# Inner seven-product forms for three aggregation products, and attention's side work in two blocks a unit

## The chip, the cores and the metric

The kernel runs on one core of a Trainium2 chip, in one launch. The metric is device time in microseconds. The kernel before takes 3564.32 us (median of three runs, 3564.18 to 3565.26). Engines are named as in the profile: PE is TensorE's matmuls, PEld its weight loads, DVE is VectorE, ACT ScalarE, POOL GpSimd, and SP the engine that issues most DMAs.

## The reference

```python
# x: (8, 2048, 256), adj: (2048, 2048), all float32
A_norm = A + eye(n)
deg = sum(A_norm, 0) + sum(A_norm, 1) - diagonal(A_norm)
A_hat = A_norm * rsqrt(deg)[:, None] * rsqrt(deg)[None, :]
agg = einsum('nm,bmd->bnd', A_hat, features)
h = relu(batchnorm(agg @ W1.T + b1, g1, be1))        # 512 columns
out = batchnorm(h @ W2.T + b2, g2, be2)              # 256 columns
x = layernorm(x + out)
qkv = x @ W                                          # 4 heads of 64
scores = einsum('bhid,bhjd->bhij', q, k) / sqrt(64) + mask   # -inf where adj == 0
x = layernorm(x + einsum('bhij,bhjd->bhid', softmax(scores), v))
```

## The kernel before

Everything is float32; one matmul is two records in the profile. There are three stages on TensorE: the aggregation with the first linear map (59 to about 1000 us), the second linear map (to about 1222 us), and attention (to the end).

**Aggregation.** The transposed adjacency is kept in SBUF in quarters `T[k, (i, j)]` of 128 x 8 x 512: i and j name halves of the 2048 nodes (contraction and output), and k counts the two 512-column slices of each half (`HT` is 8, `NK` 2, `CH` 512). A unit is (k, a pair of batches b and b + 1, d): d is the half of x's 256 columns. There are 16 units, d innermost; the two units of one (k, b) are called a pair here. In a unit the two batches and the two contraction halves make a 2 x 2 block product, done with seven products instead of eight: `product` (L360 ff.) runs 8 matmuls of 128 x 512 into one PSUM tile of the pool `psa` (four buffers). The stationary sides are the loaded x tiles `S[v, i, j]`, scaled on POOL by `scale` (L333), and their sums `S[v, 1]` to `S[v, 4]` (`s1` to `s4`, L346 to L358, on POOL). The moving sides are the quarters and their sums `T[k, 2]` to `T[k, 4]` (`t2` to `t4`, L371 to L379, on DVE, once for each k). ACT copies the first product out of PSUM, DVE adds the others, POOL multiplies the results by a row of 1/sqrt(deg) (`dbc`). x tiles and sums lie in places `x0` to `x8` (`Form`), given out in the order in which they came free.

After the d = 1 unit, `linear` (L404 ff.) does the first linear map for the two batches, again with seven products: for batch b + 1 at once, for batch b after the next unit's first product (`later`). Its forms (`linear_form`, L402) are made on POOL. The results lie in two tiles h0 and h1 and go to DRAM as `h_d`.

At the change of k (`turn`) the other four quarters are fetched from DRAM, the mask of one quarter and the sums t1 to t4 are made on DVE. `mask_of` writes the 0/1 mask of a quarter to DRAM three more times for each k.

**Attention.** 64 units (batch, pair of heads, 512 query rows) of 16 steps. In each step TensorE does the scores of three steps ahead (L933, four 64x64 matmuls) and the weighting of the values of this step (L963, four more); DVE adds the mask (L945), ACT takes the exponential (L951), and POOL adds the exponentials up (L973 as DMA, L975, L984, L986). Between these, side work is put in at steps given by hand, `at_step(unit, step, function)`: the sums of the unit before (`finish_sums`, L1004), their transposition (L1018), the turning of the output (`finish_turn`, L1031), q, k and v projections (L867, L881) of coming units, and for the next batch the transposition of y and x (`norm` L801, `turn` L830). A task with a whole-number step comes before the mask and the exponential of its step, one with a fraction after them.

**Order.** On all five engines (four in attention) instructions stay in the order in which the program writes them. An instruction that waits holds up all that stand behind it on its engine, on SP's queue of DMAs too.

Of the kernel before, what the change touches and what calls it, by code (L numbers as in the profile page):

```python
# [26 lines left out]
def tile_gcn_then_masked_attention(  # L27
# [15 lines left out]
    nc = tc.nc  # L43
# [88 lines left out]

    HT = NT // 2
# [23 lines left out]
    free = [f"x{i}" for i in range(9)]  # L157
# [24 lines left out]
    def mask_of(k, ij):  # L182

        i, j = ij
        m8 = bp.tile([P, HT, CH], U8, name="m8")
        nc.vector.tensor_scalar(m8, T[k, ij], 0.0, None, op0=ALU.is_equal)
        if i == j:
            for q in range(TPC):
                m = k * TPC + q
                nc.vector.tensor_copy(  # L190
                    m8[:, m, q * P : (q + 1) * P], mdiag[:, i * HT + m, :]
                )
        mask_out(k, ij, m8)
# [4 lines left out]
    with tc.tile_pool(name="bt7", bufs=1, side="right") as bp7, tc.tile_pool(  # L198
# [7 lines left out]
        m8 = bp.tile([P, HT, CH], U8, name="m8")  # L206
# [92 lines left out]
        mask_out(0, (0, 1), m8)  # L299

# [3 lines left out]
    with tc.tile_pool(  # L304
        name="psa", bufs=4, space=PSUM
    ) as psa, tc.tile_pool(name="psh", bufs=4, space=PSUM) as psh, tc.manual_schedule(engines=ALL4):
        for j in range(2):
            lp.tile([P, NH, CH], F32, name=f"h{j}")
# [95 lines left out]
        def linear(k, b, ag, i):  # L404

            cs = [(b + i) * NCH + j * NK + k for j in range(2)]
            lo, hi = (lp.tile([P, NH, CH], F32, name=f"h{j}") for j in range(2))
# [7 lines left out]
            def plus(h, f, p, u):  # L415
                nc.vector.scalar_tensor_tensor(
                    h[:, f, :], p, b1s[:, f : f + 1], u, op0=ALU.add, op1=ALU.add
                )

            for s, p in products((0, 0), ag[i, 0][:, 0, :]):  # L420
                nc.scalar.copy(lo[:, 2 + s, :], p)  # L421
            linear_form(ag, i, 3)
            for s, p in products((0, 1), ag[i, 0][:, 1, :]):
                plus(lo, s, p, lo[:, 2 + s, :])
            linear_form(ag, i, 4)
            for s, p in products(2, G[i, 2]):
                nc.vector.tensor_add(hi[:, s, :], p, lo[:, 2 + s, :])
            for s, p in products(3, G[i, 3]):
                nc.vector.tensor_add(hi[:, 2 + s, :], p, hi[:, s, :])
            for s, p in products((1, 1), G[i, 4]):  # L430
                plus(lo, 2 + s, p, hi[:, 2 + s, :])
            nc.sync.dma_start(h_d[cs[0]], lo)
            for s, p in products(1, G[i, 1]):
                plus(hi, 2 + s, p, hi[:, 2 + s, :])
                nc.vector.tensor_add(hi[:, s, :], p, hi[:, s, :])
            for s, p in products(4, ag[i, 1][:, 1, :]):
                plus(hi, s, p, hi[:, s, :])
            nc.sync.dma_start(h_d[cs[1]], hi)
            for c, h in zip(cs, (lo, hi)):
                for f in range(NH):  # L440
                    nc.vector.bn_stats(st1[:, f, c, :], h[:, f, :])
# [9 lines left out]
        nc.gpsimd.tensor_sub(W1[4], W1[0, 1], W1[2])  # L451
        ag = None
        for v, (k, b, d) in enumerate(units):
# [9 lines left out]

            def do_p6():
                p6 = product(S[v, 2], T[k, 2])
                nc.vector.tensor_add(u2, p6, u1)

# [5 lines left out]
            if not last:  # L473
                nb, nd = units[w][1:]
                S[w, 0, 0] = load_form(nb, 0, nd)
                S[w, 1, 0] = load_form(nb + 1, 0, nd)
                S[w, 1, 1] = load_form(nb + 1, 1, nd)
# [10 lines left out]
            if turn:  # L488
                fetch(k + 1, (0, 1), 4)
# [3 lines left out]
            if first:  # L493
                p3 = product(S[v, 4], T[k, (1, 1)])
                do_p6()
            if not last:
                S[w, 0, 1] = load_form(nb, 1, nd)
                for ij in ((0, 0), (1, 0), (1, 1)):
                    scale(w, *ij)
            if turn:  # L500
                fetch(k + 1, (1, 1), 2)
            if d and not last:
                for i in range(2):
                    linear_form(ag, i, 1)
            p7 = product(S[v, 3], T[k, 3])
            nc.vector.tensor_add(u3, p7, u2)
            if turn:
                mask_of(k + 1, (0, 1))
                t1 = T[k + 1, (0, 1)]
                nc.vector.tensor_sub(t1, t1, T[k + 1, (0, 0)])  # L510
            if not (last or turn):
                s1(w)
                s2(w)
                s3(w)
            p4 = product(S[v, 1, 1], T[k, 4])
            nc.vector.tensor_add(c21, p4, u3)
            nc.gpsimd.tensor_mul(c21, c21, dbc[0][:, 0, :])
            if turn:
                fetch(k + 1, (1, 0), 6)
                t2(k + 1, 5)  # L520
            if not last:
                scale(w, 0, 1)
                if not turn:
                    s4(w)
            p5 = product(S[v, 1], T[k, (0, 1)])
            nc.vector.tensor_add(c22, p5, u3)
            nc.vector.tensor_add(u2, p5, u2)
            nc.gpsimd.tensor_mul(c22, c22, dbc[0][:, 1, :])
            if d and not last:
                linear_form(ag, 1, 2)  # L530
            if turn:
                t3(k + 1, 1)
            if not first:
                p3 = product(S[v, 4], T[k, (1, 1)])
            nc.vector.tensor_add(c12, p3, u2)
            nc.gpsimd.tensor_mul(c12, c12, dbc[0][:, 1, :])

            n = v % (len(units) // NK)
            if n in (2, 4, 6):
                mask_of(k, ((0, 0), (1, 0), (1, 1))[n // 2 - 1])  # L540
            if last:
                break
            if d:
                linear(k, b, ag, 1)
                linear_form(ag, 0, 2)
                if turn:
                    t4(k + 1, 3)
                    s1(w)
                    s2(w)
                later = [lambda k=k, b=b, ag=ag: linear(k, b, ag, 0)]  # L550
                if turn:
                    later += [lambda w=w: s3(w), lambda w=w: s4(w)]
# [18 lines left out]
        for name, size in (  # L571
            ("h1", [P, NH, CH]), ("dbc", [P, 2, CH]), ("w1f", [P, 4, H // 2])
        ):
            t = lp.tile(size, F32, name=name).rearrange("p a b -> p (a b)")
            for i in range(size[1] * size[2] * 2 // N):
                tx = t[:, i * N // 2 : (i + 1) * N // 2].rearrange("p (t d) -> p t d", d=D)
                nc.sync.dma_start(
                    tx, x[0, len(x0) * CH : (len(x0) + 1) * CH].rearrange("(t p) d -> p t d", p=P)
                )
                x0.append(tx)  # L580
        wt = lp.tile([P, NH, CH], F32, name=f"h0")
        w2s = wt[:, :2, :].rearrange("p a b -> p (a b)").rearrange("p (f o) -> p f o", f=NH)
        w2f = wt[:, 2:, :].rearrange("p a b -> p (a b)").rearrange(
            "p (n f o) -> p n f o", n=4, f=2
        )
        nc.sync.dma_start(w2s, w2t.rearrange("(c p) f -> p c f", p=P))
# [3 lines left out]
        def w_half(i, j):  # L590
            return w2s[:, 2 * j : 2 * j + 2, i * P : (i + 1) * P]

        W = {ij: w_half(*ij) for ij in HALVES}
        W[1], W[2], W[3], W[4] = (w2f[:, n] for n in range(4))
# [172 lines left out]
    class Layer1Input:  # L767
# [27 lines left out]

        def turn_y(self, b, c, half, pm):
# [41 lines left out]
        def emit_stats(self, b, c, half):  # L838
# [14 lines left out]
        def project(self, b, hp, c, which, k_on_act=False):  # L853
# [10 lines left out]
            pm = self.psum.tile([P, CH], F32, name="pm")  # L864
# [34 lines left out]
    def attention():  # L899


        with tc.tile_pool(
# [178 lines left out]

            per_b = HP * NCH
            for u in range(NU):
                b, hp, c = units[u]
                at_step(u + 1, 6, finish_sums, u)
                at_step(u + 1, 10, finish_turn_sums, u)
                at_step(u + 1, 10.2, finish_turn, u)
                at_step(u + 1, 10.3, finish, u, 0)
                at_step(u + 1, 11.1, finish, u, 1)
                if u == NU - 2:  # L1090
                    for half in range(2):
                        at_step(u + 1, 11.3 + half, inp.emit_stats, b, c, half)
                        at_step(u + 1, 14 + half, inp.emit, b, c, half)
                    at_step(u + 1, 12.5, inp.root, b, c)
                elif u == NU - 1:
                    for half in range(2):
                        at_step(u + 1, 10.4 + half, inp.emit_stats, b, c, half)
# [4 lines left out]
                    at_step(u + 1, 10.45, count_bad)  # L1102
                elif hp == HP - 1:
                    for half in range(2):
                        at_step(u + 1, 12.5 + 1.5 * half, inp.emit_stats, b, c, half)
# [5 lines left out]
            PROJECT = (0.2, 6.1, 10.1)  # L1111

            def project_at(u, b, hp, c):
                for w in range(3):
                    at_step(u, PROJECT[w], inp.project, b, hp, c, w)

            for b in range(B):
                u0 = b * per_b
                if b:
                    project_at(u0, b, 0, NCH - 1)  # L1120
                for c in range(NCH):
                    project_at(u0 + 1 + c, b, 1, c)
# [7 lines left out]
                    at_step(u, 6.2, inp.norm, b + 1, c, 0)  # L1130
                    at_step(u + 1, 0.1, inp.norm, b + 1, c, 1)
                    at_step(u + 1, 3, inp.root, b + 1, c)
                    for half in range(2):
                        at_step(u + 1, 7 + half, inp.apply, b + 1, c, half)
                        at_step(u + 1, 13 + 0.2 * half, inp.turn, b + 1, c, half)
# [13 lines left out]
            for c in (2, 3):  # L1149
                at_step(c - 1, 3.1, inp.project, 0, 0, c, 0)  # L1150
# [76 lines left out]
    def attention_with_maxima():  # L1227

        with tc.tile_pool(name="full", bufs=2) as ap_, tc.tile_pool(
# [9 lines left out]
            for b in range(B):  # L1239
# [55 lines left out]
                for c in range(NCH):  # L1295
                    for half in range(2):
                        inp.emit_stats(b, c, half)
# [53 lines left out]
```

## Time and profile before

| what | us |
|---|---|
| median of three runs | 3564.32 |
| profiled execution: device time | 3566.12 |
| profiled execution: span | 3564.3 |
| L363 aggregation products, PE busy | 774.8 |
| L412 first linear map, PE busy, its three largest groups | 76.8, 76.7, 26.3 |
| L933 scores / L963 values, PE busy | 1062.9 / 1074.2 |
| L867 and L881 projections, PE busy | 250.8 and 125.1 |
| 59 to 995 us: POOL busy / DVE busy | 434 / 338 |
| 1247 to 3552 us: POOL busy / DVE busy | 1698 / 1576 |

A group's line reads: line, engine, operation, output <- inputs, shapes, count | busy us, mean ns of one | idle before it and who ended that. A timeline line reads: start, duration (both us), engine, line, operation, count. Rows of PE in the timeline overlap a little, since matmuls are pipelined; the distance of two starts is what a group takes.

### The profile page before, as it was taken

What the parts mean: (1) busy time and instruction counts of PE and PEld (TensorE: products, weight loads), DVE (VectorE), ACT (ScalarE), POOL (GpSimd) and SP (SyncE); (2) the same over time, 40 slices, a digit from 0 to 9 for tenths busy, and PEclk for the clock granted to TensorE, in tenths of its full rate; (3) what the DMA queues carried; (4) which work ended last, traced back from release to release, by engine and by line L of the source; (5) the groups of instructions that cost most, each with busy time, mean ns of one, the idle gap of its engine ahead of it and who ended that gap; (6) DMA issues with size and microseconds to landing.
All of it is one profiled execution on the core that took longest, in us unless ns stands there. A gap on an engine that the chain in (4) does not pass through costs nothing. (4 is left out here: it accounts for less than half of the span.)

```text
span 3564.3 us, 55375 instructions
## 1 busy us (share of the span) xinstructions
PE 3527.1 (99%) x22483; PEld 1461.0 (41%) x22483; DVE 2113.4 (59%) x3128; ACT 1575.4 (44%) x1952; POOL 2330.5 (65%) x1588
## 2 busy tenths in 40 slices
PE   8999999999999999999999999999999999999998
PEld 5444444444444433433343433343443334343332
DVE  6224343442346656766766776676676676677666
ACT  5000000000045455665665565565566566566555
POOL 4544364435357656777777787777677777777777
PEclk9999999999999999999999999999999999999999
DMA  9122342231256445666575566566656556555655
GB/s 342 54 77 76 95 153 78 71 95 39 84 217 249 156 84 109 128 126 123 110 149 117 115 129 134 113 133 129 118 124 136 114 117 145 115 117 115 122 107 121
DMA packets 197577, 440.16 MB, mean 123 GB/s; under 512 B 14128, under 2 KB 121152, under 8 KB 186944
## 3 DMA queue, kind: packets, MB, share of 16 engines
q0 software_dynamic: 64656, 239.37, 35.3%
q1 hardware_dynamic: 132048, 196.11, 16.2%
q8 instruction: 178, 2.92, 0.3%
q10 hardware_dynamic: 608, 1.06, 0.1%
q14 instruction: 87, 0.71, 0.1%
HBM read 126.62 MB, written 75.51 MB: 57 GB/s over the span
## 5 line engine op out<-in xcount | busy, mean ns | idle before, releaser
L945 DVE SCALAR_TENSOR_TENSOR prob<-mask,st 128x1024 f32<-128x1024 uint8 x1024 | 1239.0, 1215 | 434.6 <-PE st L933 358.6
L951 ACT ACTIVATE prob<-prob 128x1024 f32<-128x1024 f32 x1024 | 1081.2, 1056 | 913.4 <-DVE prob L945 836.6
L963 PE MATMUL out_ps<-prob,v 64*64 64x512 f32 x8192 | 1074.2, 595 | 3.6 <-DVE ot L991 2.6
L933 PE MATMUL st<-qt,kt 64*64 64x512 f32 x8192 | 1062.9, 589 | 0.1
L986 POOL TENSOR_TENSOR acc<-acc,prob 128x1024 f32<-128x1024 f32 x317 | 825.6, 2604 | 5.5 <-DMA prob<-prob 0.6
L363 PE MATMUL pa<-t,x 128*128 128x512 f32 x1792 | 774.8, 594 | 2.8 <-ACT t L239 2.8
L973 POOL DMA_DIRECT2D prob<-prob x447 | 403.6, 928 | 565.4 <-PE out_ps L963 453.4
L933 PEld LDWEIGHTS st<-qt,kt 64*64 64x64 f32 x8192 | 312.5, 133 | 566.7 <-issue 527.0
L363 PEld LDWEIGHTS pa<-t,x 128*128 128x128 f32 x1792 | 341.4, 191 | 432.9 <-issue 428.7
L963 PEld LDWEIGHTS out_ps<-prob,v 64*64 64x64 f32 x8192 | 290.8, 133 | 542.4 <-issue 470.5
L975 POOL TENSOR_TENSOR acc<-acc,prob 128x1024 f32<-128x1024 f32 x126 | 298.1, 2366 | 7.5
L867 PE MATMUL pm<-x1t,wq 128*128 128x512 f32 x512 | 250.8, 613 | 0.7 <-ACT x1t L836 0.7
L492 POOL TENSOR_TENSOR ag<-ag,dbc 128x512 f32<-128x512 f32 x16 | 20.2, 1264 | 314.7 <-DVE ag L491 287.2
L472 ACT COPY ag<-pa 128x512 f32<-128x512 f32 x16 | 9.4, 588 | 450.0 <-PE pa L363 434.0
L421 ACT COPY h<-ph 128x512 f32<-128x512 f32 x28 | 16.4, 585 | 416.7 <-PE ph L412 416.7
L984 POOL TENSOR_TENSOR acc<-prob 128x1024 f32<-128x1024 f32 x64 | 170.7, 2667 | 3.0 <-DMA prob<-prob 3.0
L762 ACT ACTIVATE x<-x,ln_nm,ln_rs 128x256 f32<-128x256 f32 x256 | 137.6, 586 | 7.5 <-POOL ln_nm L758 7.5
L1039 DVE SCALAR_TENSOR_TENSOR x<-pm,ri,x 128x64 f32<-128x64 f32 x512 | 109.6, 277 | 43.6 <-PE pm L1031 43.6
L867 PEld LDWEIGHTS pm<-x1t,wq 128*128 128x128 f32 x512 | 86.9, 189 | 118.2 <-issue 111.6
L881 PE MATMUL pm<-wq,x1t 128*128 128x128 f32 x1024 | 125.1, 275 | 0.0
L881 PEld LDWEIGHTS pm<-wq,x1t 128*128 128x128 f32 x1024 | 119.4, 192 | 2.5 <-ACT x1t L836 1.7
L991 DVE TENSOR_TENSOR ot<-out_ps,ot 128x512 f32<-128x512 f32 x64 | 44.3, 692 | 123.9 <-ACT ot L990 123.9
(158 smaller groups left out, 2863.5 us busy)
## 6 DMA issues: line engine op xcount, KB each, us to landing
prob<-prob POOLq DMA_DIRECT2D x447, 512.0 KB, 4.9
x<-in_x_dram SPq DMA_DIRECT2D x92, 512.0 KB, 6.5
h_d<-h SPq DMA_DIRECT2D x28, 1024.0 KB, 4.3
t<-h_d SPq DMA_DIRECT2D x28, 1024.0 KB, 8.2
a<-in_adj_dram SPq DMA_DIRECT2D x16, 1024.0 KB, 5.4
y_d<-ag SPq DMA_DIRECT2D x32, 512.0 KB, 2.7
out_dram<-x SPq DMA_DIRECT2D x31, 512.0 KB, 6.6
yt<-y_d SPq DMA_DIRECT2D x28, 512.0 KB, 3.3
```

The source lines that it names most:

```text
L363: nc.tensor.matmul(pa, s.t[:, m, :], t[:, m, :], start=(m == 0), stop=(m == HT - 1))
L762: nc.scalar.activation(self.t[:, i, :], self.t[:, i, :], AF.Identity, bias=self.nm[:, i : i + 1], scale=self.rs[:, i : i + 1],)
L867: nc.tensor.matmul(pm, wq[:, d, wcols], xt[:, d, cols], start=(d == 0), stop=(d == ND - 1))
L881: nc.tensor.matmul(pm[:, j * P : (j + 1) * P], xt[:, d, t * P : (t + 1) * P], wq[:, d, wcols], start=(d == 0), stop=(d == ND - 1),)
L933: nc.tensor.matmul(st[r * HD : (r + 1) * HD, h, :], kt[hs, j * P + r * HD : j * P + (r + 1) * HD], qt[hs, cols], start=True, stop=True,)
L945: nc.vector.scalar_tensor_tensor(p, mask[:, j, cols][:, None, :].to_broadcast([P, 2, CH]), MASKED, st, op0=ALU.mult, op1=ALU.add,)
L951: nc.scalar.activation(probs[g], probs[g], AF.Exp)
L963: nc.tensor.matmul(outs[u][hs, r, :], inp.qkv[b, hp][2][rs, j, hs], probs[g][rs, h, :], start=(j == 0), stop=(j == NT - 1),)
L973: nc.gpsimd.dma_start(probs[g - 1], probs[g], accum_op=ALU.add)
L975: nc.gpsimd.tensor_add(accs[u], accs[u], probs[g])
L984: nc.gpsimd.tensor_add(accs[v], probs[g - 7], probs[g - 5])
L986: nc.gpsimd.tensor_add(accs[v], accs[v], probs[g - 5])
```

## The change

**Aggregation.** The four products p1, p6, p2 and p7 of a unit stay. The products with T4, T(0,1) and T(1,1) are no longer done in each unit, but once for both units of a pair, after the d = 1 unit's p7: rows are the two d halves, the contraction of 1024 is cut in two, and the 512 columns in two, which gives a 2 x 2 block product again, done with seven products of four matmuls of 128 x 256 (class `Inner`). For each of the three, in turn:

- DVE makes the moving sums t2, t3 and t4 (128 x 1024 elements each; t4 takes t2's place after p6),
- POOL makes four stationary sums x1 to x4 (128 x 512 each) from the forms of both units,
- the seven results are put together by ACT (one copy) and DVE in a place `sums`, and DVE adds that (128 x 1024) to the tiles of `ag` that need it: one, two and one times.

The sums for the next of the three are made while one runs. The forms of d = 0 are kept until then, so there are ten places `x0` to `x9`; the mask no longer has a tile of its own, but uses such a place or `wide0`. The tiles h0 and h1 become two tiles `wide` and four `narrow`, which hold the inner sums and, in `linear`, h; h goes to DRAM in six pieces. Loading, scaling and making the next unit's forms are moved; the first unit has its p3 no longer ahead of p6; at the turn, the mask and t1 and t2 are made in slices inside the inner runs, and t3 and t4 afterwards.

```diff
+            def run(self, place, follower=None, extra=()):
...
+                p1 = product(self.a(0, 0), self.b(0, 0))
+                nc.scalar.copy(c21, p1)
+                p2 = product(self.a(0, 1), self.b(1, 0))
+                nc.vector.tensor_add(c11, p2, c21)
+                more()
+                p6 = product(self.x2, self.y2)
+                self.t4()
+                nc.vector.tensor_add(c12, p6, c21)
+                p5 = product(self.x1, self.b(0, 1))
+                more()
+                if follower:
+                    follower.s12()
+                p7 = product(self.x3, self.y3)
+                nc.vector.tensor_add(c22, p7, c12)
+                nc.vector.tensor_add(c12, p5, c12)
+                if follower:
+                    follower.t2()
+                    follower.s3()
+                p4 = product(self.a(1, 1), self.y2)
+                nc.vector.tensor_add(c21, p4, c22)
+                nc.vector.tensor_add(c22, p5, c22)
+                more()
+                p3 = product(self.x4, self.b(1, 1))
+                nc.vector.tensor_add(c12, p3, c12)
+                for dst, src in self.targets:
+                    nc.vector.tensor_add(dst, c, src)
+                more()
+                if follower:
+                    follower.t3()
+                    follower.s4()
...
             def do_p6():
                 p6 = product(S[v, 2], T[k, 2])
                 nc.vector.tensor_add(u2, p6, u1)
+                if not d:
+                    for ij in ((0, 0), (1, 0), (1, 1)):
+                        scale(w, *ij)
+                    s1(w)
+                elif not last:
+                    load(1, 0)
...
             p2 = product(S[v, 0, 1], T[k, (1, 0)])
             nc.vector.tensor_add(c11, p2, u1)
             nc.gpsimd.tensor_mul(c11, c11, dbc[0][:, 0, :])
             if first:
-                p3 = product(S[v, 4], T[k, (1, 1)])
                 do_p6()
+            if not d:
+                s2(w)
+                scale(w, 0, 1)
...
+                inner[0].t2()
+                inner[0].t3()
+                inner[0].s12()
+                inner[0].s3()
+                inner[0].s4()
             p7 = product(S[v, 3], T[k, 3])
             nc.vector.tensor_add(u3, p7, u2)
+            if not d:
+                s3(w)
+                s4(w)
...
+            if not last:
+                for ij in ((0, 0), (1, 0)) if turn else ((0, 0), (1, 0), (1, 1)):
+                    scale(w, *ij)
+            inner[0].run(sums.t, inner[1], extra[:4])
...
+            by_rows((1, 0), 0)
+            if turn:
+                fetch(k + 1, (1, 0), 6)
+            elif not last:
+                s1(w)
+                s3(w)
+            inner[1].run(sums.t, inner[2], extra[4:8])
+            by_rows((1, 1), 1)
+            if not last:
+                linear_form(ag, 1, 1)
+                linear_form(ag, 1, 2)
+                if turn:
+                    scale(w, 1, 1)
+                scale(w, 0, 1)
             if not (last or turn):
+                s2(w)
+                s4(w)
+            inner[2].run(sums.t, None, extra[8:])
...
+            linear(k, b, ag, 1)
+            by_rows((0, 1), 1)
```

`by_rows` is two multiplications on POOL (128 x 512 each); `more` takes the next slice of the turn's work.

**Attention.** For all units but the last few, the side work on TensorE goes into two steps: step 6 (sums, key projection, transposition of the sums, value projection, turning of the output) and step 15 (x turned, y transposed and added, query projection). The key projection and the transposition of y write into buffers of the scores' PSUM pool.

```diff
+            def key_projection(b, hp, c):
+                st = ps_s.tile([P, 2, CH], F32, name="st")
+                inp.project(b, hp, c, 1, pm=st[:, 0, :])
...
+                if u + 1 < BARE:
+                    at_step(u + 1, 6.2, finish_turn_sums, u)
+                    at_step(u + 1, 6.4, finish_turn, u)
+                    at_step(u + 1, 6.5, finish, u, 0)
+                    at_step(u + 1, 7.1, finish, u, 1)
...
-            PROJECT = (0.2, 6.1, 10.1)
...
+                at_step(u, 15 if last else 15.2, inp.project, b, hp, c, 0)
+                at_step(u, 6.1, key_projection, b, hp, c)
+                at_step(u, 6.3, inp.project, b, hp, c, 2)
...
-                    at_step(u, 6.2, inp.norm, b + 1, c, 0)
-                    at_step(u + 1, 0.1, inp.norm, b + 1, c, 1)
+                    at_step(u, 15.1, norm, b + 1, c)
...
-                        at_step(u + 1, 13 + 0.2 * half, inp.turn, b + 1, c, half)
+                        at_step(u + 1, 15.15 if half > c else 15, inp.turn, b + 1, c, half)
```

## The prediction

> **What bounds the kernel now.** I read the page first (busy shares, slices), then the groups by line, then TensorE's own waits, then the timeline of single stretches.
>
> ```profile
> span 3564.3 us, 55375 instructions
> PE 3527.1 (99%) x22483; PEld 1461.0 (41%) x22483; DVE 2113.4 (59%) x3128; ACT 1575.4 (44%) x1952; POOL 2330.5 (65%) x1588
> ...
> L363 PE MATMUL pa<-t,x 128*128 128x512 f32 x1792 | 774.8, 594 | 2.8 <-ACT t L239 2.8
> ```
>
> TensorE is the bound from end to end: its own waits, added over the whole trace, come to some 23 us. Time can only fall if TensorE's instructions take less, and it rises by every wait that the change puts in front of one. L363 is the aggregation. It runs at peak: in the timeline one product (8 matmuls, 16 records) takes 6.86 us, 0.42875 us a record. Sixteen units of seven products are 768 us of the 775.
>
> The attention timeline shows what a block of side work costs:
>
> ```profile
> 2003.15 1.04 PE L963 MATMUL out_ps<-prob,v 64*64 64x512 f32 x8
> 2004.01 1.04 PE L933 MATMUL st<-qt,kt 64*64 64x512 f32 x8
> 2004.98 0.44 PE L1018 MATMUL pm<-ident,sm 128*128 128x128 f32 x2
> 2005.25 1.95 PE L881 MATMUL pm<-wq,x1t 128*128 128x128 f32 x16
> 2007.04 0.60 PE L1031 MATMUL pm<-ident,ot 128*128 128x128 f32 x4
> 2007.57 1.09 PE L963 MATMUL out_ps<-prob,v 64*64 64x512 f32 x8
> 2008.48 1.04 PE L933 MATMUL st<-qt,kt 64*64 64x512 f32 x8
> ```
>
> The first column is the start. Score and value groups follow each other every 0.86 us. Before the block the step is 0.97, after it 0.91: entering and leaving costs 0.11 + 0.05 = 0.16 us, whatever lies in it. L1004 alone adds 0.73 us, L867 alone 2.08, both in one block 2.65: joined, they save 0.16 too.
>
> DVE and POOL look half idle, but they block each other. This is the turn from k = 0 to 1, the one place where DVE now has long operations with two SBUF inputs; first DVE, then POOL:
>
> ```profile
> 507.19 4.88 DVE L371 TENSOR_TENSOR t<-t,t 128x4096 f32<-128x4096 f32 x1
> ...
> 513.32 6.03 DVE L375 TENSOR_TENSOR t<-t,t 128x4096 f32<-128x4096 f32 x1
> ```
>
> ```profile
> 507.76 5.45 POOL L517 TENSOR_TENSOR ag<-ag,dbc 128x512 f32<-128x512 f32 x1
> 513.17 1.90 POOL L333 TENSOR_TENSOR x<-x,dinv 128x1024 f32<-128x1024 f32 x1
> ```
>
> L517 takes 1.27 us elsewhere; here it ends 1.14 us after L371 does. L375 takes 4.42 us undisturbed; here it starts only when L333 ends. One blocks the other for a whole instruction, and they alternate.
>
> **What the Trainium skill says.** "SBUF — State Buffer", section "Who interferes with whom": a DVE instruction with two SBUF inputs contends with a GpSimd instruction that reads SBUF, and the second fully blocks. The lines above agree (4.2 and 1.6 us of blocking). One with a PSUM input does not contend: L402 keeps its 1.27 us beside DVE's additions from PSUM. "TensorE: Matmul & The Clock Gate", section "Back-to-back issue gap": N/2.4 + 2.5 ns warm. Our 512-column matmul is two records of two passes: 1024/2.4 + 2.1 = 428.75 ns, which agrees.
>
> **Part 1, the inner products: matmuls.** Per pair of units (d = 0, 1) six products of 6.86 us become three runs of seven products of four 256-column matmuls. No record shows 128x256 against 128 rows. From below: half of 428.75, 1.715 us a product. From above: a line through 111.9 ns (L881, 128 columns: 1.79 us for 16) and 428.75 gives 217.5 ns a record, 1.74 us. The page's gap gives 1.727 as an estimate. Weight loads last 190 ns, but L881 sustains one every 112 ns, so they don't bind. I take 1.73: a run is 12.1 us for 13.7, and 24 runs give -39 us (-37 to -41).
>
> **Part 1, its queues.** Take an ordinary d = 1 unit, with time 0 at the end of p2. TensorE then has p7 (6.86), 21 inner products (36.3), six matmuls of linear (6 x 0.858 = 5.15), and then needs form 3 of linear: 48.3 us. POOL can't start early, since the multiply of c11 waits for p2 and DVE's addition (1.0 us). In program order it then has: that multiply, 12 inner forms, 4 row scalings, forms 1, 2 and 3 of linear (20 operations of 512 elements at 1.22 us from start to start, 24.4); four scalings of the next unit (1.87, 7.5); s1, s3, s2, s4 (2.30, 9.2); dependent starts (0.7). With the 1.0 that is 42.8 us, which would fit. But DVE now has 13 operations with two SBUF inputs of 1024 elements: t2 and t3 three times, t4 three times, four additions into ag, 1.14 us each (a quarter of 4.42 plus the fixed part). POOL is busy throughout, so nearly each delays it: 14.8 less some 1.8 of overlap at the handovers, 13.0. Sum 55.8 against 48.3: TensorE waits 7.5 us per pair. Walking the queues places it: some 0.2 at run 2's first product (the PSUM buffer of p5 is freed late, because DVE's t2 stands in front), 2.5 at run 2's p6 (x2 stands behind row scaling, s1 and s3), the rest at the product of linear that reads form 3, behind s2 and s4. A lock half hidden in idle time of POOL gives 2; POOL waking 0.1 us late at each of its 28 operations gives 10. Six ordinary pairs: +45 (12 to 60).
>
> The turn pair has no s1 to s4 in this stretch (-9.2), but ten DVE slices of 1.14 (+11.4), and DVE's t4 is then late too: +10. The last pair prepares nothing: 0. The first unit loses its cover:
>
> ```profile
> 93.30 1.26 POOL L492 TENSOR_TENSOR ag<-ag,dbc 128x512 f32<-128x512 f32 x1 [27.59 <-DMA dbc<-dinv_d]
> 94.52 5.60 POOL L333 TENSOR_TENSOR x<-x,dinv 128x1024 f32<-128x1024 f32 x3
> ```
>
> POOL stands until dbc lands at 93.3, and only then scales unit 1's input. Now unit 0 has seven products until 110. With four, TensorE is done at 69.0 + 3 x 6.86 = 89.6 and waits for the first scaling at 96.5 (6.9), then for s2 at 104.9 (1.5): +8.5. Between, in d = 0 units, POOL has ended s4 some 26 us into the unit and is idle, so nothing is carried on. The loads moved on SP all have over 7 us before their scaling, except unit 0's third, which waits for the mask's transfer out of the reused form; dbc covers that. Linear's h in six pieces instead of two halves moves the same bytes: 0.
>
> Part 1: -39 + 45 + 10 + 8.5 = +24.5.
>
> **Part 2, attention.** The timeline has 223 blocks. Afterwards units 0 to 60 have two each (steps 6 and 15), the start and the last three units some 15: 137. 86 x 0.16 = -14. L801's wait for ACT's copy of the sums, 2.6, goes. An L867 that directly precedes L963 takes 0.1 longer in some blocks; up to 5 goes with those. I take -19 (-12 to -24). In the step-6 block, ACT's copy of the sums (0.37) lies beside the key projection (1.8), so L1018 isn't late. At step 15 the query projection (1.8) covers the copy and addition of ot (0.58 + 0.69), as at step 0 now. A projection in a score buffer shifts the rotation by one; the scores that follow need a buffer whose mask DVE began over 5 us earlier. DVE's four additions (0.86) after the block end before the next scores arrive (1.7). The remaining moves (statistics, root, emit) lie on engines with slack.
>
> Sum: 3564.3 + 24.5 - 19 = 3570. The profiled execution was 3566.1 us of device time, 1.8 around its span; the median of the runs is 3564.3, so the sum is put on that.
>
> **Rivals.** The measurement can tell about 0.2%, 7 us.
> 1. The locks don't reach TensorE, because DVE's forms fall where POOL waits for a product. For: without locks POOL ends its 42.8 us with 5 to spare. Against: it would be idle only that much. Ordinary pairs then cost nothing, the turn 3: -39 + 8.5 + 3 - 19 gives 3518; half of it 3541.
> 2. Slower, by POOL's queue in the inner runs: if each wait also moves DVE's additions, four PSUM buffers don't decouple, and run 1 and 2 wait at p1, p6 and p4. At 12 us a pair: +27, 3597. It decides from 8 us a pair, where the sum passes 0.2%.
> 3. Attention's POOL falls behind. From step 7 to 15 there is no block now, and one DMA plus one accumulation take 3.44 us for 3.43 of TensorE. By my walk the last sum is ready 2.6 us before step 6 needs it. If it is 1 us late in each unit: 3564 + 24.5 - 19 + 60 = 3630.
>
> **Numbers.** Main case 0.45, own range 3556 to 3584 (0.03 faster, 0.24 same, 0.18 slower). Rival 1: 0.30. Rival 2: 0.18. Rival 3 and worse: 0.07. Faster 0.33, same 0.24, slower 0.43. Range 3530 to 3600: about 0.1 is left out on each side.
>
> **What would show it.** Records of 128x256 every 0.216 us; TensorE's waits at L412 on POOL of 4 to 5 us and at the inner p6 on POOL of 2 to 3, in six pairs; POOL operations there stretched by 1.1 us; one wait of 7 us near 90 us; attention shorter by 19 us, with two blocks a unit. I am wrong if the inner forms on POOL keep 1.27 us while DVE works, or if attention's first scores of a unit wait.

## The result, and the profile after

The changed kernel takes 3567.51 us (median of 20 runs, 3563.36 to 3569.68), the kernel before 3564.22 on the same chip: a ratio of 1.0009, 95% interval 1.0002 to 1.0016. That is +3.3 us, less than 0.2%: no change that counts, and it is the sum of two large effects of opposite sign.

The page of the kernel after, with the lines that answer to those of before (L378 is the old L363):

```profile
span 3566.6 us, 57179 instructions
PE 3481.9 (98%) x23059; PEld 1591.6 (45%) x23059; DVE 2350.3 (66%) x3349; ACT 1592.5 (45%) x1976; POOL 2542.9 (71%) x1684
...
L378 PE MATMUL pa<-t,x 128*128 128x512 f32 x1024 | 447.5, 597 | 10.0 <-POOL x L348 6.0
```

TensorE has 45 us less to do (3527.1 to 3481.9), and the span is 2.3 us longer: it now waits, where it did not. DVE and POOL have each gained over 200 us of busy time. The waits of TensorE in the kernel after (line waited in, what for: us in total, times, longest):

```profile
PE ph L429 <- POOL ag L417: 18.6, 6, 4.2
PE pa L532 <- POOL narrow L510: 14.5, 6, 2.4
...
PE pa L378 <- POOL x L348: 6.0, 1, 6.0
PE pa L532 <- DVE wide L502: 4.7, 2, 2.4
PE pa L532 <- DVE wide L499: 4.5, 2, 3.2
```

Two waits come six times each, once in each ordinary pair: an inner p6 (L532) for x2 of POOL, and the product of `linear` (L429) that reads form 3. One is in the first unit (L378), and the DVE ones are in the turn pair. Cut into stages on TensorE (from the first aggregation product to the first linear map of the last pair, which both kernels do alike; from the first value product to the last):

| | before | after | difference |
|---|---|---|---|
| aggregation with the first linear map | 941.1 | 972.5 | +31.4 |
| of which TensorE's waits inside the stage | 0.2 | 49.5 | +49.3 |
| attention | 2290.8 | 2262.0 | -28.8 |
| attention: blocks of side work | 223 | 134 | -89 |

This is an ordinary pair in the kernel after, first TensorE (start, duration, line, operation, count, and the wait ahead of it), then DVE, then POOL:

```profile
279.84 3.13 PE L532 MATMUL pa<-wide,narrow 128*128 128x256 f32 x8 [2.40 <-POOL narrow L510]
282.76 2.48 PE L532 MATMUL pa<-t,narrow 128*128 128x256 f32 x8
285.08 1.89 PE L532 MATMUL pa<-wide,narrow 128*128 128x256 f32 x8
...
298.08 3.43 PE L429 MATMUL ph<-ag,w1f 128*128 128x512 f32 x4 [2.50 <-POOL ag L417]
```

```profile
274.48 4.19 DVE L562 TENSOR_TENSOR ag<-x,ag 128x1024 f32<-128x1024 f32 x2
278.59 2.28 DVE L499 TENSOR_TENSOR wide<-wide,t 128x1024 f32<-128x1024 f32 x1
```

```profile
277.66 2.12 POOL L510 TENSOR_TENSOR narrow<-narrow,x 128x512 f32<-128x512 f32 x1
279.75 2.25 POOL L514 TENSOR_TENSOR narrow<-x,x 128x512 f32<-128x512 f32 x1
281.95 1.27 POOL L518 TENSOR_TENSOR narrow<-x,narrow 128x512 f32<-128x512 f32 x1
...
291.04 3.34 POOL L365 TENSOR_TENSOR x<-x,x 128x1024 f32<-128x1024 f32 x1
294.45 2.35 POOL L373 TENSOR_TENSOR x<-x,x 128x1024 f32<-128x1024 f32 x1
296.76 1.26 POOL L417 TENSOR_TENSOR ag<-g,ag 128x512 f32<-128x512 f32 x1
```

Read the three together. A free inner form takes POOL 1.27 us (L518); the two ahead of it last 2.12 and 2.25. L510 begins while DVE's two additions into `ag` run (L562, to 278.67), and L514 while DVE's t3 runs (L499, to 280.87): each gets through only when DVE's operation has ended, and t3 in turn is held up by L510. x2 (L510) is ready at 279.78, and p6 starts at 279.84. Later s2 and s4 (L365, L373) stand ahead of form 3 (L417, the last line), which ends at 298.02; the product that reads it starts at 298.08. POOL shows no gap: its queue sets both times.

There is a second loss in the TensorE rows that no list of waits names. The p6 at 279.84 takes 2.92 us from start to start and the next product 2.32, where undisturbed ones take 1.73. The windows of the same kernel show why (stretch, length, busy us of PE, PEld, DVE, ACT and POOL, the granted TensorE clock, DMA share, GB/s):

```profile
273.80:277.40 3.60, 3.60 (x17) 2.85 (x15) 3.49 (x4) 0.00 (x0) 3.60 (x2) 1.00 0.00 0
279.80:282.76 2.96, 2.92 (x8) 2.37 (x9) 1.40 (x2) 0.00 (x0) 2.96 (x2) 0.62 0.00 0
282.76:285.08 2.32, 2.32 (x9) 1.97 (x8) 1.63 (x2) 0.00 (x0) 2.32 (x2) 0.74 0.00 0
...
298.08:301.34 3.26, 3.26 (x4) 1.48 (x5) 0.69 (x1) 0.00 (x0) 3.26 (x3) 0.55 0.00 0
```

The clock is full before the wait, 0.62 and 0.74 after it, and 0.55 after the second wait; between them products take their 1.73 us again. In this pair that is (2.92 - 1.73) + (2.32 - 1.73) + (3.26 - 1.72) = 3.3 us. It is not so in every pair. These are all six (us; "lost" is what the next two products take beyond 1.73 or 1.72 each):

| p6 starts at | wait ahead of it | then lost | wait for form 3 | then lost |
|---|---|---|---|---|
| 155.12 | 2.43 | 0.1 | 4.21 | 2.5 |
| 279.84 | 2.40 | 1.8 | 2.50 | 1.5 |
| 403.65 | 2.42 | 1.7 | 2.62 | 0.1 |
| 654.28 | 2.42 | 0.1 | 4.21 | 1.8 |
| 778.39 | 2.44 | 1.8 | 2.51 | 0.1 |
| 900.77 | 2.42 | 1.8 | 2.51 | 1.7 |

Four of the twelve waits (those with 0.1 behind them) left the clock full, though all four were longer than the 2.40 that did not. Together the six pairs lose 15 us in this way. Where p6 keeps its clock, the wait for form 3 is 4.21; where it does not, that wait is about as much shorter as p6 and its successor are slower. Finer windows show the difference between the p6 at 279.84 and the one at 155.12:

```profile
277.13:280.54 3.41, 1.00 (x5) 0.65 (x4) 3.41 (x2) 0.37 (x1) 3.33 (x3) 1.00 0.00 0
280.54:283.95 3.41, 3.41 (x9) 2.72 (x9) 1.60 (x3) 0.00 (x0) 3.41 (x3) 0.50 0.00 0
...
150.83:154.25 3.42, 1.86 (x9) 1.30 (x7) 3.42 (x3) 0.22 (x1) 3.34 (x2) 1.00 0.00 0
154.25:157.66 3.41, 2.54 (x12) 2.26 (x13) 2.74 (x3) 0.15 (x1) 3.41 (x3) 1.00 0.00 0
```

PE is busy for 1.00 of 3.41 us in the first window, and the clock is 0.50 in the whole of the next one; at 155.12 the wait falls into two windows and the clock stays at 1.00. The last section says what decides it. The first unit loses 3.2 in the same way (10.02 us for a product of 6.86 behind its wait of 5.96), the turn 2.5. So the aggregation's +31.4 is -39.1 for the shorter runs, +49.3 of waits and +21 of slow matmuls (15, 3.2 and 2.5), with under 1 us left over.

The block of side work in attention, in the kernel after:

```profile
2050.92 1.04 PE L1128 MATMUL st<-qt,kt 64*64 64x512 f32 x8
2051.89 0.64 PE L1199 MATMUL pm<-acc,ones 128*32 128x256 f32 x8
2052.46 1.98 PE L1062 MATMUL st<-x1t,wq 128*128 128x512 f32 x4
2054.28 0.38 PE L1213 MATMUL pm<-ident,sm 128*128 128x128 f32 x2
2054.50 1.95 PE L1076 MATMUL pm<-wq,x1t 128*128 128x128 f32 x16
2056.29 0.60 PE L1226 MATMUL pm<-ident,ot 128*128 128x128 f32 x4
2056.82 1.09 PE L1158 MATMUL out_ps<-prob,v 64*64 64x512 f32 x8
```

It adds 2056.82 - 2050.92 = 5.90, less the step of 0.86, and 0.05 in the step behind it: 5.09 us. Before, the same work lay in two blocks of 2.65 and 2.75. The join saves 0.31, not 0.16.

### The profile page after: what moved, and what is told of

It is laid out like the page before. It is cut to its first block, busy times and chain, and to the rows that moved or that the text cites. A ratio compares the mean times of both kernels' runs of the same rounds, so it can differ in the third digit from the quotient of the medians.

```text
span 3566.6 us, 57179 instructions
## 1 busy us (share of the span) xinstructions
PE 3481.9 (98%) x23059; PEld 1591.6 (45%) x23059; DVE 2350.3 (66%) x3349; ACT 1592.5 (45%) x1976; POOL 2542.9 (71%) x1684
## 5 line engine op out<-in xcount | busy, mean ns | idle before, releaser
L1158 PEld LDWEIGHTS out_ps<-prob,v 64*64 64x64 f32 x8192 | 305.6, 133 | 544.2 <-issue 490.2
L378 PE MATMUL pa<-t,x 128*128 128x512 f32 x1024 | 447.5, 597 | 10.0 <-POOL x L348 6.0
L378 PEld LDWEIGHTS pa<-t,x 128*128 128x128 f32 x1024 | 195.8, 192 | 258.4 <-issue 243.7
L348 POOL TENSOR_TENSOR x<-x,dinv 128x1024 f32<-128x1024 f32 x60 | 128.4, 2161 | 104.4 <-DMA x<-in_x_dram 104.4
L538 ACT COPY x<-pa 128x256 f32<-128x256 f32 x24 | 8.9, 372 | 391.3 <-DVE ag L562 215.2
L1062 PE MATMUL pm<-x1t,wq 128*128 128x512 f32 x272 | 132.5, 610 | 2.6 <-ACT x1t L1030 2.4
L438 ACT COPY wide<-ph 128x512 f32<-128x512 f32 x28 | 16.4, 586 | 237.5 <-PE ph L429 237.5
L626 POOL TENSOR_TENSOR ag<-ag,dbc 128x512 f32<-128x512 f32 x16 | 30.4, 1897 | 126.6 <-DVE ag L625 101.8
```

The lines of the kernel that those rows point to most:

```text
L348: nc.gpsimd.tensor_mul(t, t, dinv[:, j * HT : (j + 1) * HT][:, :, None].to_broadcast([P, HT, P]),)
L378: nc.tensor.matmul(pa, s.t[:, m, :], t[:, m, :], start=(m == 0), stop=(m == HT - 1))
L1062: nc.tensor.matmul(pm, wq[:, d, wcols], xt[:, d, cols], start=(d == 0), stop=(d == ND - 1))
L1158: nc.tensor.matmul(outs[u][hs, r, :], inp.qkv[b, hp][2][rs, j, hs], probs[g][rs, h, :], start=(j == 0), stop=(j == NT - 1),)
```

## The experiments

### Each part alone

The first kernel has only the attention part, the second only the aggregation part.

```diff
-            PROJECT = (0.2, 6.1, 10.1)
...
+                at_step(u, 6.1, key_projection, b, hp, c)
+                at_step(u, 6.3, inp.project, b, hp, c, 2)
```

> The kernel before with the change's attention part alone; the aggregation is the one before. If the parts add, and the timeline's 532 us of side work against 504 after is all that attention gains: 28 us less than before, 3536. If my sum of 19 (blocks joined at 0.16 each) was right and the rest of the 28 comes from elsewhere: 3545. If attention's gain in the full change is only there because the aggregation shifts something: no change, 3564. TensorE should show 134 blocks of side work.

```diff
+            inner[0].run(sums.t, inner[1], extra[:4])
...
+            inner[1].run(sums.t, inner[2], extra[4:8])
...
+            inner[2].run(sums.t, None, extra[8:])
```

> The kernel before with the change's aggregation part alone. If the parts add: 31 us more than before, 3595, with the aggregation's span 972 us as in the full change, 49 us of waits on TensorE in it and a granted clock of 0.98. If they do not add: nearer to 3567.

Measured, beside 3563.62 for the kernel before: attention alone 3534.21 (ratio 0.9918, 0.9905 to 0.9932), -29.4; aggregation alone 3596.02 (1.0093, 1.0078 to 1.0109), +32.4. Their sum, +3.0, is the +3.3 of both together: the parts do not touch each other. The stages agree: the attention takes 2261.9 in the first and 2290.8 in the second, the aggregation 939.7 and 971.3. So the attention part gains half as much again as I had counted, and the aggregation part loses more.

### The lock: one SBUF operand for DVE

The t sums and the additions into `ag` keep their sizes, engines, order and places, but their second operand comes from a PSUM tile, which two transpositions on TensorE fill in each pair. That leaves part of the computation out: the subtrahends of t2, t3 and t4, and the inner sums in `ag`.

```diff
-                nc.vector.tensor_sub(self.y2, self.b(1, 1), self.b(0, 1))
+                nc.vector.tensor_sub(self.y2, self.b(1, 1), one())
...
-                nc.vector.tensor_sub(self.y2, self.b(1, 0), self.y2)
+                nc.vector.tensor_sub(self.y2, self.b(1, 0), one())
...
-                    nc.vector.tensor_add(dst, c, src)
+                    nc.vector.tensor_add(flat(dst), flat(src), one())
```

> The full change, but each of DVE's 13 operations per pair with two SBUF inputs reads its second operand from PSUM (an identity block put there by two transpositions, 0.3 us a pair), with the same count, size, place in the queue and waits. This leaves the inner sums of T and the addition into ag out of the result. Theory of the lock: POOL's inner forms go back to 1.27 us, TensorE's waits on POOL in the inner runs and in linear (14.5 and 18.6 us in the full change) go to under 3 us together, and the slow clock behind them goes too, some 3 us a pair: about 3520. Rival, POOL's queue is too long by itself: the waits stay within 1 us a pair of what they are, 3560 to 3570.

Measured: 3509.66 (0.985, 0.9835 to 0.9865), 58 us below the kernel after. The first of the four inner forms among the groups on POOL, first in the kernel after, then in this one (line, operation, shapes and count; busy us, mean ns of one; idle before):

```profile
L509 POOL TENSOR_TENSOR narrow<-x 128x512 f32<-128x512 f32 x24 | 45.9, 1913 | 6.0 <-PE pa L532 5.9
```

```profile
L517 POOL TENSOR_TENSOR narrow<-x 128x512 f32<-128x512 f32 x24 | 31.3, 1304 | 22.8 <-PE pa L540 22.8
```

The form drops from 1913 ns to 1304, and POOL gets idle time in front of it (22.8 us for 6.0): it is no longer the bound. TensorE's longest wait on another engine in this kernel:

```profile
PE pa L378 <- POOL x L348: 6.0, 1, 6.0
```

Both six-fold waits are gone; the first unit's remains, as it has nothing to do with the lock. POOL's busy time in the aggregation falls from 640.9 to 551.7 us. Over the 104 DVE operations that were changed (24 runs with three sums, eight pairs with four additions) that is 0.86 us each; the prediction had put 1.0. Undisturbed, one of these operations lasts 1.21 us with either operand; in the kernel after they take 1.46 to 2.20 on average, since POOL holds them up too. So the edit took away the lock and not the work: the lock, and nothing else about the added instructions, makes POOL's operations longer. This agrees with the Trainium skill, "SBUF — State Buffer", section "Who interferes with whom", on which the prediction leaned. Whether that reaches TensorE depends on what else stands in POOL's queue, as the next runs show. The time fell further than the waits of the ordinary pairs explain, since the turn's waits went with them.

### Taking the waits away

If POOL's queue is what sets the two waits, moving s1 to s4 of the next unit out of the inner runs must remove them without touching any lock. In ordinary pairs they now stand behind `linear`, as they did in the turn pair.

```diff
-            elif not last:
-                s1(w)
-                s3(w)
...
-            if not (last or turn):
-                s2(w)
-                s4(w)
...
+            s1(w)
+            s2(w)
+            later += [lambda f=f, w=w: f(w) for f in (s3, s4)]
```

> The full change with only s1 to s4 moved behind linear in every pair; the turn and the first unit stay as in the change. Theory: POOL's stretch falls by 9.2 us, from 55.8 to 46.6 by my sum, under the 48.3 that TensorE takes, so the waits of all six ordinary pairs (33 us) and their slow clock (17) go: 3517. If the lock itself, not the length of the queue, held up x2 and form 3, half of the waits stay: 3540.

Measured: 3518.85 (0.9875, 0.986 to 0.989), 48.7 below the kernel after, 8.1 us for each ordinary pair. No wait on `narrow` or on form 3 is left; those of the first unit (6.0) and of the turn pair (L502 4.7, L499 3.3) are. A second kernel also takes on the turn and the first unit: the turn's slices are spread over the runs more thinly, the last ones behind `linear`; the multiply of c11 that stands waiting for `dbc` in the first unit goes behind s4, and the place of the first mask is given back a little later.

```diff
-            inner[0].run(sums.t, inner[1], extra[:4])
+            inner[0].run(sums.t, inner[1], extra[:2])
...
-            nc.gpsimd.tensor_mul(c11, c11, dbc[0][:, 0, :])
             if first:
                 do_p6()
+            else:
+                nc.gpsimd.tensor_mul(c11, c11, dbc[0][:, 0, :])
...
+                if first:
+                    nc.gpsimd.tensor_mul(c11, c11, dbc[0][:, 0, :])
```

> The full change with POOL's s1 to s4 of the next unit moved behind linear in every pair (as the change does at the turn), the slices at the turn spread over the three runs and linear, and in the first unit c11's multiply behind the scalings, with a free place for the third load. All of the result is computed. If TensorE's 49 us of waits and the 20 or so of slow clock behind them are the whole of what the aggregation lost: 3567 - 65 = 3500, with under 8 us of waits in the aggregation. If the waits only move to other products: above 3540.

Measured: 3508.76 (0.9848, 0.9834 to 0.9861). The whole computation is in it, so this is a version that beats both kernels: 1.5% below the one before. Its aggregation takes 912.3 us, 8.7 of them waits; the 3500 expected would have needed these to go too. The further 10 us against the previous kernel are the first unit and the turn. The longest of them on another engine:

```profile
PE pa L531 <- DVE wide L501: 3.0, 2, 2.4
```

The wait of 6.0 for the first scaling is gone, and what is late next is DVE in the turn.

### The clock: dummies in the waits

Do the slow matmuls behind the waits cost all of the 15 us that they add up to in the six pairs? TensorE gets matmuls whose result is overwritten, five ahead of run 2's p6 and three ahead of the product that reads form 3, in the six ordinary pairs: the waits are filled, and no queue moves.

```diff
+                    for m in range(warm):
+                        nc.tensor.matmul(
+                            p, self.a(0, 0)[:, m % M, :], self.b(0, 0)[:, m % M, :],
+                            start=True, stop=True,
+                        )
                     for m in range(M):
```

> The full change, with dummy matmuls where TensorE waits in six pairs: five of 128x256 ahead of p6 in the third inner run (2.2 us for a wait of 2.4), three of 128x512 ahead of linear's product with form 3 (2.6 us for waits of 2.5 to 4.2). Their results are overwritten; nothing is left out. Theory: the slow matmuls behind each wait come from the granted clock, which falls because TensorE stood still; kept busy, it holds 1.00 there and some 17 us go: 3550. Rival: they are slow because the operands or PSUM are in use elsewhere: no gain, 3567 or some us more.

Measured: 3562.0 (0.9994, 0.9985 to 1.0002), 5.5 us below the kernel after, with an uncertainty of some 3. The same pair on TensorE:

```profile
277.31 1.99 PE L542 MATMUL pa<-wide,narrow 128*128 128x256 f32 x8 [0.26 <-POOL narrow L515]
279.14 1.89 PE L542 MATMUL pa<-t,narrow 128*128 128x256 f32 x8
...
291.20 2.74 PE L431 MATMUL ph<-g,w1f 128*128 128x512 f32 x6
295.58 1.98 PE L434 MATMUL ph<-ag,w1f 128*128 128x512 f32 x4 [1.65 <-POOL ag L417]
297.40 1.88 PE L434 MATMUL ph<-ag,w1s 128*128 128x512 f32 x4
```

L431 are the second dummies; the first stand ahead of 277.31. p6 now takes 1.83 from start to start, for 2.92, the product behind form 3 takes 1.82 (for 3.26). The granted clock is 1.00 in all six pairs (99.7 to 529.7 and 540 to 1024 us; only the turn lies between): it stays up, and the waits were what lowered it. But the gain is small, and the times say why. From run 1's first product (261.73 after, 259.19 here) to the product that reads form 3 (298.08 and 295.58) it is 36.35 us after and 36.39 here. POOL's queue sets that distance, so slow matmuls ahead of form 3 only take the place of waiting. Only the slow ones behind form 3, 1.4 us in this pair and 7 in all six, are lost on top, and the 5.5 gained fits that. The clock is real, and I had put too large a price on it.

### Attention: what a joined block saves

The step-6 block is split again: the key projection stays with the sums, the rest goes to step 10 as before.

```diff
-                    at_step(u + 1, 6.2, finish_turn_sums, u)
-                    at_step(u + 1, 6.4, finish_turn, u)
+                    at_step(u + 1, 10, finish_turn_sums, u)
+                    at_step(u + 1, 10.2, finish_turn, u)
...
-                at_step(u, 6.3, inp.project, b, hp, c, 2)
+                at_step(u, 10.1, inp.project, b, hp, c, 2)
```

The statistics that read the result are moved behind it, to steps 12.2 and 12.4.

> The full change with the block of step 6 split as in the kernel before: sums and key projection at step 6, transposition of the sums, value projection and turning of the output at step 10. The same work in 59 more blocks. At 0.16 a block, as I reckoned: 3577. At 0.31, the difference of the blocks in the timelines (2.65 + 2.75 against 5.09): 3586.

Measured: 3597.56 (1.0092, 1.0077 to 1.0108), 30 us above the kernel after. There are 194 blocks with 522.4 us of side work, for 134 with 504.2: 60 more blocks cost 18.2, 0.30 each. From their two halves on TensorE:

```profile
2024.75 1.98 PE L1062 MATMUL st<-x1t,wq 128*128 128x512 f32 x4
2026.67 1.09 PE L1158 MATMUL out_ps<-prob,v 64*64 64x512 f32 x8
...
2033.70 0.44 PE L1213 MATMUL pm<-ident,sm 128*128 128x128 f32 x2
2033.97 1.95 PE L1076 MATMUL pm<-wq,x1t 128*128 128x128 f32 x16
```

The key projection takes 2026.67 - 2024.75 = 1.92 here, in front of a 64x64 value product; in the joined block it takes 1.82. The transposed sums take 0.27 behind a 64x64 product, 0.22 behind the projection. With the 0.16 of entering and leaving these are 0.31.

The other 12 us of the 30 are not blocks. The waits of this kernel have one that the kernel after does not show:

```profile
PE st L1128 <- DVE prob L1140: 4.6, 28, 0.3
```

In 27 steps the distance is 1.20 us for 0.86, some 9 us, where scores wait for DVE's mask of the buffer that they need. I moved DVE's statistics with the block, which may be the cause; that was not tried apart, and it stays open.

## Why the prediction came out as it did

The predicted sum was +5.5 (to 3570), the measured difference +3.3. It was right for the reason it gave in the aggregation, and it was helped by errors that cancel.

| term | predicted | measured | from |
|---|---|---|---|
| inner matmuls | -39 | -39.1 | 1.727 us a product, 24 runs |
| ordinary pairs, POOL's queue | +45 | +48.7, slow clock included | forms moved out of them |
| turn and first unit | +18.5 | +22.8 | what is left of +32.4 |
| attention | -19 | -29.4 | attention alone |
| sum | +5.5 | +3.0 | |

- **The inner matmuls** were right to a tenth of a microsecond a run: half of the known record plus the fixed part.
- **POOL's queue with the lock** was right in kind and place, and near in size. The walk gave 2.5 us at run 2's p6 and 4.8 at the product with form 3. Measured are 2.40 to 2.44, and 4.21 in the two pairs in which p6 kept its clock; in the four others 2.50 to 2.62, with 1.7 to 1.8 of slow matmuls ahead in the same gap. So the gaps come to 6.6 us a pair for 7.5, the POOL operations having lengthened by 0.86 each for 1.0. The slow matmuls behind form 3, 1.3 a pair on average, were no term of my sum: it put the clock at nothing. That 8.1 a pair came out so near to 7.5 is in part luck, as a gap put too long and a missing term offset each other.
- **The first unit and the turn.** 6.9 was predicted for the first scaling, 5.96 measured; 1.5 for s2, 0.39 measured; the slow clock behind it (3.2) was missing. The turn has waits of 9.2 where 10 was predicted, and 2.5 of slow matmuls that were no term. No run takes the two apart.
- **Attention** was the step that failed, in its size. "86 x 0.16 = -14" priced a join by what lies around a block. I had seen that L867 in front of L963 takes longer and allowed "up to 5" for it, as a side note, where it belongs to every join that puts something between a projection and the 64x64 products. 89 blocks went, at 0.31 each. The 2.6 us of L801's wait was mostly a false gain too: the wait for ACT's copy of the sums went, but the query projection now waits 1.7 in attention for ACT's copy of the turned x. (TensorE's waits before, put at "some 23", add up to 25; nothing rests on it.)
- **The rivals.** Without locks, 3518 was predicted, and the kernel without them ran at 3509.66: as a mechanism that is confirmed, as a forecast it was refuted, since the locks do reach TensorE. Slower by 12 us a pair did not come: 8.1 are above the 8 from which it was to decide, and without the larger gain of attention the result would have been some 13 us slower than before. POOL falling behind in attention did not come either: all of TensorE's waits in attention are 4.9 us.

## What to carry to other kernels

Fewer matmuls pay only if the queues that feed them end in time: count the engine's instructions up to the one that TensorE needs, with the time that another engine's two-SBUF operations add to them, and see what stands ahead that is not needed yet. Here four forms for the next unit, moved behind the deadline together with a few moves at the turn and the start, turned the aggregation part's +32 us into some -26 (-55 for the kernel, less the -29 of attention). A change that moves the time little may be two large ones: run each part alone first.

## What the runs showed of the hardware

- The granted clock was 1.00 or 0.50, and in all nine traces, from the start of the aggregation on, the distances between its changes are multiples of 3.41 us: they cut the time into stretches of that length. What counted was how much TensorE waited within one such stretch. Between 57 and 3400 us, all 35 stretches at full clock with 2.03 us of waiting or more were followed by one at 0.50; of the stretches with up to 1.96 none was (63 of them had over 1.2); of four in between, three were. So the wait of 2.40 that lay inside one stretch (277.13 to 280.54) halved the clock, and the one of 2.43 that the end of a stretch cut into 1.56 and 0.87 did not. This is read from the traces; no run moved a wait in order to try it. The Trainium skill, "TensorE: Matmul & The Clock Gate", section "HAM oscillation — how this bites in real kernels", names gaps above some 3.4 us; the measurement decides, and here shorter ones did it.
- That loss was on the path only behind the last wait that the late queue set (5.5 us came back of 15). Ahead of it, slow matmuls filled time in which TensorE would have waited: 36.35 us with them, 36.39 without.
- A 128x512 projection took 1.91 to 1.92 us between 64x64 matmuls, or with the sums ahead of it and 64x64 matmuls behind, and 1.82 where transpositions of 128x128 stood directly behind it (1.81 with them directly ahead): the switch cost more than the distances around a block show.
